# Two tiles for the image of the first pass, other homes for the second pass's first buffers

## The chip, the cores and the metric

The kernel runs on one core of a Trainium2 chip. The metric is device time in microseconds (us), the median of three runs. The engines named below are PE (TensorE, matrix products), DVE (VectorE), ACT (ScalarE), POOL (GpSimd) and SP (SyncE, which here only issues DMAs). "PEld" in the profile is the load of a matmul's stationary operand.

## What is computed

Two layers over `x` of shape (8, 256, 64, 64) in float32, eight images of 256 channels and 4096 pixels:

```python
# layer 0: attention of all pixels to 256 reduced positions
xr = conv(x, w_sr, stride 4x4)            # 16x16 positions
xr = layer_norm(xr)
q = w_q @ x;  k, v = split(w_kv @ xr)     # 8 heads of 32
out = softmax(q k^T / sqrt(32)) v
x = x + gamma * (w_out @ out)

# layer 1: linear attention on qkv and on a convolved copy
qkv = w_qkv @ x                           # 768 channels
agg = grouped_1x1(depthwise_5x5(qkv))     # 96 groups of 8
for each head of 8 channels in (qkv, agg):
    q, k = relu(q), relu(k);  kv = sum over pixels of k (v, 1)
    att = (q kv) / (q sum(k) + 1e-15)
p = batch_norm(w_proj @ att)              # 512 -> 256
return x + p
```

## The kernel before

There are three passes. Each writes to scratch memory in DRAM what the next one reads.

**The first pass** does layer 0 and the `qkv` product of layer 1. It goes over the eight images b, each in 8 strips of 512 pixels. An image's `x` is one tile `x_b` of 128 partitions x 2 x 4096 numbers, 32 KB in each partition; there are two such homes, used in turn (`xpools`, L583), so `x_{b+2}` lies where `x_b` lay. `load_x` (L600) queues eight loads, one for each strip (`load_strip`, L605). `keys_values` (L675) reduces the image by 1024 matmuls of `sr` over all pixels (L687), a line in the profile. `queries` (L759) and `added` (L842) work on a strip: `added` writes layer 0's result over `x_b` and stores it to `x2` in DRAM (L850, two stores for each strip). After two strips, a group, `differences` (L856) and the products of `qkv` (L891) make the `qkv` of the group; its parts go out by way of `stage` tiles to `planes` (L924), and by way of `turned` tiles to `k` (L934) and `v` (L939). An image has four groups, so the last group's stores come after strip 7's `x2` stores.

**The second pass** does the depthwise convolution and the sums over pixels, in 64 units; unit u stands for a half t, a quarter k of the half and an image b, with b running fastest. Unit u needs the tiles

- `d1_u` and `d0_u`, 578 KB each, from `planes` (`load_cells`, L1126);
- `kq_u`, 512 KB, from `k`, and `vq_u`, in four loads of 384 KB, from `v` (`load_tokens`, L1133 and L1143);
- `w1` and `w0`, the convolution's weights, four loads of 384 KB each for eight units (`load_weights`, L1120).

`paired` makes `c1_u` from `d1_u` by two subtractions on DVE (L1153, L1154) and a copy on POOL (L1157); `positive` (L1196) takes the relu of `kq_u` on ACT and reduces it on POOL (`red_raw`). `convolve(u, 1, i)` makes three banks `cv1_u_2`, `cv1_u_0`, `cv1_u_1` with 8 matmuls each (L1213), which become `r1_u` by `both` (L1220, ACT), `s` (L1228, DVE) and a relu (L1229, ACT). `summed_raw` (`raw_u`, L1238) multiplies `kq_u` and `vq_u`, `summed` (`sums_u`, L1255) `r1_u` and `vq_u`; `ended` (`few_u`, L1298) and `ended_raw` (L1285) finish them with the reduced tiles `red_agg_u` and `red_raw_u`. `convolve(u, 0, i)` (with L1217) does the same for the queries and `applied` (`ng_u`, L1329) multiplies them by the sums; `stored` (L1349) writes the result `att_u`. Work on a unit reaches over four turns of the main loop (L1353): `cv1_u` in its own, `sums` one later, `cv0` two later, `ng` three later.

Before its loop the pass queues `w1` of the first eight units, `d1_0`, `kq_0`, `vq_0`, then `w0`, then the constants `taps` (1152 KB), `mix`, `msk`, `rep_w` and `pix` (L1169) with `d1_1` between them, then `d0_0`. `kq_1` and `vq_1` are queued in the loop's first turn.

**The third pass** does the normalisation of layer 1 on the first half of its heads (`n`, L1526), transposes both halves (`at`, L1544) and projects (`p`, L1562), in 64 steps. It begins with a mask, `vec` and `wproj` (the projection's weights), the sums `kvp` of the first images (L1436), and `raw` (L1458) and `xs` (L1467) for each step; the first `n`, `at` and `p` mix with the second pass's last units.

**What sets the order.** Nothing writes the order of instructions out by hand: a scheduler places them on the engines by priorities that follow the program, and an instruction can only be placed when the memory of the tile that it writes has been released. All loads and stores stand in one queue that SP works off in order: an issue that waits holds back everything behind it. A DMA also waits for the one eight places before it to land. Tiles of the second pass lie on memory that the first pass has used: a pool of the second pass takes addresses in the order in which the pools are opened (L1097 and after), so a tile's home decides which tile of the first pass must be through before its load can stand in the queue, and the load's place in the queue follows from that. Two small tiles at the end of the first pass, `both` and `fits` (L1073 to L1081), test the range of some numbers for a slower path that these inputs do not take.

Of the kernel before, what the change touches and what calls it, by code (L numbers as in the profile page):

```python
# [574 lines left out]
def first_pass(ctx: ExitStack, tc: tile.TileContext, a, fine, planes, x2d, kd, vd, wtd):  # L575
# [2 lines left out]

    const = ctx.enter_context(tc.tile_pool(name="const", bufs=1))
    nilpool = ctx.enter_context(tc.tile_pool(name="nilpool", bufs=1))  # L580
    xpools = [ctx.enter_context(tc.tile_pool(name=f"xpool{i}", bufs=1)) for i in range(2)]
    keys = ctx.enter_context(tc.tile_pool(name="keys", bufs=1))
    two = ctx.enter_context(tc.tile_pool(name="two", bufs=2))  # L583
    made = ctx.enter_context(tc.tile_pool(name="made", bufs=1))
    rest = ctx.enter_context(tc.tile_pool(name="rest", bufs=2))
    halves = ctx.enter_context(tc.tile_pool(name="halves", bufs=1))

# [4 lines left out]
        return psum.tile([P, 512], F32, tag="mm", name=name, bufs=5)  # L592

    def load(src, name):
        consts[name] = const.tile(list(src.shape), F32, tag=name, name=name)
        nc.sync.dma_start(consts[name], src)

    consts, x_tiles = {}, {}

    def load_x(b):  # L600
        x_tiles[b] = xpools[b % 2].tile([P, 2, HW], F32, tag="x", name=f"x_{b}")
        for s in range(NG):
            load_strip(b, s)

    def load_strip(b, s):  # L605
        src = a.xp[b].rearrange("(c p) n -> p c n", p=P)
        cols = slice(s * QB, (s + 1) * QB)
        nc.sync.dma_start(x_tiles[b][:, :, cols], src[:, :, cols])

    def load_consts():  # L610
        for n, src in (
# [61 lines left out]
    kks, vvs = {}, {}  # L673

    def keys_values(b):  # L675
        xt = x_tiles[b]
        ln = lambda name: keys.tile([P, 2, NK], F32, tag="ln", name=f"{name}_{b}", bufs=3)
        xr = ln("xr")

# [2 lines left out]
        for f, tap in taps:  # L682
            w = keys.tile([P, 2, C], F32, tag="wsr", name=f"wsr_{b}_{f}", bufs=4)
            nc.sync.dma_start(w, a.w_sr[:, :, tap])
            for ci in range(2):
                for oc in range(2):
                    nc.tensor.matmul(  # L687
                        ps[:, oc],
                        w[:, ci, oc * P : (oc + 1) * P],
                        xt[:, ci, f * NK : (f + 1) * NK],  # L690
                        start=(f == ci == oc == 0),
                        stop=(f == R * R - 1 and ci == 1),
                        skip_group_check=True,
                    )
            yield
# [60 lines left out]
    def queries(b, s, c):  # L756
        ps = bank(f"q_{b}_{s}_{c}")
        for ci in range(2):
            nc.tensor.matmul(  # L759
                ps,  # L760
                consts["wq"][:, ci, c * P : (c + 1) * P],
                x_tiles[b][:, ci, s * QB : (s + 1) * QB],
                start=(ci == 0),
                stop=(ci == 1),
            )
        qs = two.tile([P, QB], F32, tag="q", name=f"q_{b}_{s}_{c}")
        nc.scalar.copy(qs, ps)
        return qs
# [71 lines left out]
        late.append(noted)  # L840

    def added(b, s, att, oc):  # L842
        xt, cols = x_tiles[b], slice(s * QB, (s + 1) * QB)
# [3 lines left out]
        nc.vector.scalar_tensor_tensor(  # L847
            xt[:, oc, cols], ps, consts["gam"][:, 0:1], xt[:, oc, cols], ALU.mult, ALU.add
        )
        nc.sync.dma_start(x2d[b][oc * P : (oc + 1) * P, cols], xt[:, oc, cols])  # L850

    quarters = {}

    def differences(b, g):  # L856
        xt = x_tiles[b]
        x = xt[:, :, 2 * g * QB : 2 * (g + 1) * QB].rearrange("p c (h n) -> p c h n", h=2)
# [123 lines left out]


    weights = conv_weights()
    x_tiles[0] = xpools[0].tile([P, 2, HW], F32, tag="x", name="x_0")
    ahead = keys_values(0)
    for s in range(NG):
        load_strip(0, s)
# [81 lines left out]
        pass  # L1070


    both = const.tile([P, 2], F32, tag="both", name="both")  # L1073
    nc.vector.tensor_reduce(both, seen.rearrange("p (n k) -> p k n", k=2), AX.X, ALU.add)
    total = bank("total")[:, :2]
    nc.tensor.matmul(total, mean_w, both, start=True, stop=True)
    fits = const.tile([P, 4], F32, tag="fits", name="fits")
# [11 lines left out]
def second_pass(ctx: ExitStack, tc: tile.TileContext, a, planes, kd, vd, wtd, kvd, attd):  # L1089
    nc = tc.nc  # L1090
    B = a.x.shape[0]
    def pool(name, bufs=1):
        return ctx.enter_context(tc.tile_pool(name=name, bufs=bufs))

    const, late, mid = pool("const2"), pool("late2", 2), pool("mid2")  # L1097
    first, second, small, w_taps, pairs, sides, between, third, w_q, two = (
        pool("first2"), pool("second2"), pool("small2", 2), pool("taps2"), pool("pairs2", 2),
        pool("sides2", 2), pool("between2", 2), pool("third2"), pool("wq2"), pool("two2", 2),  # L1100
    )
    psums = {
        tag: ctx.enter_context(tc.tile_pool(name=f"psum_{tag}", bufs=1, space=bass.MemoryType.PSUM))
# [11 lines left out]
    def load_weights(u, what, g):  # L1115
        t, k, b = units[u]
        if g == 0:
            home = (third if k % 2 else first) if what else (third if k % 2 else w_q)
            wt[t, k, what] = home.tile([P, 4, 6 * P], F32, tag=f"w{what}_{k % 2}", name=f"w{what}_{t}_{k}")
        nc.sync.dma_start(wt[t, k, what][:, g], wtd[2 * what + t][:, 4 * k + g])  # L1120

    def load_cells(u, what):
        t, k, b = units[u]
        home = (second if u % 2 else first) if what else third
        d = home.tile([P, 4, (NB + 1) ** 2], F32, tag=f"d{what}_{u % 2}", name=f"d{what}_{u}")
        nc.sync.dma_start(d, planes[b, 2 * what + t][4 * k : 4 * k + 4].rearrange("g p e -> p g e"))  # L1126
        grids[u, what] = d.rearrange("p g (y x) -> p g y x", x=NB + 1)


    def load_tokens(u):  # L1130
        t, k, b = units[u]
        kq = (second if u % 2 else first).tile([P, 2, 4, P], F32, tag=f"kq_{u % 2}", name=f"kq_{u}")
        nc.sync.dma_start(  # L1133
            kq.rearrange("p a c e -> p a (c e)"),
            kd[b][4 * t + k].rearrange("a y (m i) b e -> (y m) a (i b e)", i=2),
        )
        kqs[u] = kq
        vq = (second if u % 3 else first).tile([P, 4, 6 * P], F32, tag=f"vq_{u % 3}", name=f"vq_{u}")
        v = vd[b][4 * t + k]
        row = (NB2 + 2) * P  # L1140
        for r in range(4):
            src = [[2 * row, NB], [4 * P, NB // 2], [1, 6 * P]]
            nc.sync.dma_start(vq[:, r], bass.AP(tensor=v.tensor, offset=v.offset + r * row, ap=src))  # L1143
        vqs[u] = vq.rearrange("p r (c f h e) -> p r c f h e", c=6, f=4, h=4)
# [16 lines left out]
        load_weights(0, 1, g)  # L1161
    load_cells(0, 1)
    load_tokens(0)
    for g in range(4):
        load_weights(0, 0, g)

    def load(home, src, name):
        t = home.tile(list(src.shape), F32, tag=name, name=name)
        nc.sync.dma_start(t, src)  # L1169
        return t  # L1170

    taps = load(w_taps, a.w_taps, "taps")
    load_cells(1, 1)
    mix = load(const, a.w_mix, "mix")
    msk = load(const, a.mask_h, "msk")
    rep_w = load(const, a.replicate, "rep_w")
# [24 lines left out]
    def convolve(u, what, i):  # L1201
# [14 lines left out]
                        out = out.rearrange("p (y x) -> p y x", y=NB)  # L1216
                    nc.tensor.matmul(out, m, x, start=(da == 0), stop=(da == 1))  # L1217
        if i == 2:
            both = between.tile([P, QB], F32, tag="both", name=f"both{what}_{u}")
            nc.scalar.copy(both, ps)  # L1220

            r = (sides if what else two).tile([P, 2, 4, P], F32, tag=f"r{what}", name=f"r{what}_{u}")
            state[u, what] = (r, both)
            (kts if what else qs)[u] = r
        else:
            r, both = state[u, what]
            s = sides.tile([P, QB], F32, tag="s", name=f"s{what}_{u}_{i}")
            nc.vector.tensor_add(s, ps, both)  # L1228
            nc.scalar.activation(r[:, i].rearrange("p h n -> p (h n)"), s, AF.Relu)  # L1229
# [18 lines left out]
    def summed(u):  # L1248
# [508 lines left out]
```

## Time and profile before

| | us |
|---|---|
| median of three runs | 3973.13 (3971.51 to 3975.15) |
| the profiled execution | 3977.62 |
| its span | 3975.8 |
| first pass, up to its last matmul | 2066 |
| second pass, its first `c1` to its last `ng` | 2042 to 3318 |
| third pass, to the end | 3291 to 3976 |

The mean granted clock of TensorE is 0.989 of full speed over the span. The passes overlap at their joints, as their instructions mix there.

The profile is of one execution. Its page gives busy time by engine, then the span in 40 slices, the DMA queues, the chain that ended last, the costliest groups of instructions and the DMA issues. In a timeline a line is a run of like instructions: start, length, engine, line of the code, operation, tiles, and in brackets the idle time before it and what ended it. In the list of waits a line is an engine and line, what it waited for, the total in us, how many times, and the longest. Loads of constants are counted by size:

```
vq<-v SPq DMA_DIRECT2D x256, 384.0 KB
d<-planes SPq DMA_DIRECT2D x128, 578.0 KB
x<-in_xp_dram SPq DMA_DIRECT2D x64, 512.0 KB
kq<-k SPq DMA_DIRECT2D x64, 512.0 KB
taps<-in_w_taps_dram SPq DMA_DIRECT2D x1, 1152.0 KB
mix<-in_w_mix_dram SPq DMA_DIRECT2D x1, 256.0 KB
```

### The profile page before, as it was taken

The numbers are of one execution on the slowest core, as the hardware profiler recorded it, in microseconds if no ns is written. First come the engines' busy times: TensorE is split into PE (matmuls) and PEld (weight loads), VectorE is DVE, ScalarE is ACT, GpSimd is POOL, SyncE is SP. The second block draws the span as 40 slices with busy tenths as digits, with TensorE's granted clock in tenths as the row PEclk, the third lists the DMA queues.
The fourth block names the chain that finished last, engine by engine and source line by source line (L and its number), as shares of the span: only waits on it lengthen the run. The fifth ranks groups of instructions, "written<-read, shape, count | busy, mean of one in ns | idle before, by whom it ended". The sixth has DMA issues, their size and how long they took to land. (4 is left out here: it accounts for less than half of the span.)

```text
span 3975.8 us, 70172 instructions
## 1 busy us (share of the span) xinstructions
PE 3884.2 (98%) x27074; PEld 2279.0 (57%) x27074; DVE 2267.2 (57%) x3752; ACT 1516.5 (38%) x3473; POOL 1291.5 (32%) x1394
## 2 busy tenths in 40 slices
PE   8999999999999999999988999999999998999998
PEld 4443434434344343443337888888888886555555
DVE  2567465564655646556664566666666664444444
ACT  2334344443444434444422222222222223555554
POOL 2344243342433424334433444444444430000000
PEclk9999999999999999999998999999999999999999
DMA  7655445344453444534549878878777657767674
GB/s 241 188 167 157 143 112 151 102 111 142 112 152 101 112 140 112 151 102 113 135 121 272 240 224 228 229 215 231 230 216 231 204 151 188 232 202 230 203 227 140
DMA packets 569897, 691.37 MB, mean 174 GB/s; under 512 B 60112, under 2 KB 429264, under 8 KB 565328
## 3 DMA queue, kind: packets, MB, share of 16 engines
q1 hardware_dynamic: 569552, 686.78, 60.9%
q8 instruction: 215, 3.52, 0.4%
q14 instruction: 130, 1.06, 0.1%
HBM read 412.54 MB, written 274.10 MB: 173 GB/s over the span
## 5 line engine op out<-in xcount | busy, mean ns | idle before, releaser
L809 POOL TENSOR_TENSOR e<-e,e 128x512 f32<-128x512 f32 x512 | 679.3, 1357 | 941.9 <-PE av L798 879.1
L780 ACT ACTIVATE e<-sc 128x512 f32<-128x512 f32 x1024 | 531.2, 603 | 803.1 <-PE sc L774 798.9
L1213 PE MATMUL cv<-w,c 128*128 128x128 f32 x3072 | 386.8, 280 | 11.4 <-POOL c L1157 11.0
L1213 PEld LDWEIGHTS cv<-w,c 128*128 128x128 f32 x3072 | 360.9, 193 | 42.3 <-issue 28.9
L1580 DVE TENSOR_TENSOR y<-z,xs 128x256 f32<-128x256 f32 x256 | 144.2, 652 | 312.8 <-ACT z L1571 300.1
L774 PE MATMUL sc<-q,kk 32*128 32x512 f32 x2048 | 320.1, 640 | 2.0 <-DVE part L960 1.0
L1255 PE MATMUL sums<-vq,r 128*32 128x288 f32 x4096 | 308.0, 414 | 0.0
L891 PE MATMUL qkv<-differences,combined 128*128 128x512 f32 x576 | 306.8, 624 | 0.9 <-ACT e L780 0.7
L907 DVE TENSOR_TENSOR whole<-part,qkv 128x512 f32<-128x512 f32 x256 | 175.5, 687 | 193.1 <-PE qkv L891 181.9
L798 PE MATMUL av<-e,vv 128*32 128x512 f32 x2048 | 273.1, 605 | 1.9 <-ACT att L818 1.9
L1229 ACT ACTIVATE r<-s 128x512 f32<-128x512 f32 x256 | 160.5, 627 | 299.9 <-DVE s L1228 299.7
L1571 ACT ACTIVATE z<-p,bn 128x256 f32<-128x256 f32 x256 | 133.7, 578 | 314.6 <-PE p L1562 240.4
L1217 PE MATMUL cv<-c,w 128*128 128x128 f32 x2048 | 253.4, 277 | 0.0
L1562 PE MATMUL p<-att,wproj 128*128 128x512 f32 x512 | 249.4, 609 | 1.9 <-ACT att L1545 1.9
L846 PE MATMUL o<-att,wout 128*128 128x512 f32 x512 | 234.4, 600 | 11.9 <-DVE att L831 11.9
L1220 ACT COPY both<-cv 128x512 f32<-128x512 f32 x128 | 74.9, 585 | 446.4 <-PE cv L1213 389.0
L759 PE MATMUL q<-x,wq 128*128 128x512 f32 x512 | 244.8, 600 | 0.0
L687 PE MATMUL sr<-x,wsr 128*128 128x256 f32 x1024 | 233.3, 382 | 9.3 <-DMA wsr<-in_w_sr_dram 9.3
L1562 PE MATMUL p<-agg,wproj 128*128 128x512 f32 x512 | 242.3, 596 | 0.0
L1217 PEld LDWEIGHTS cv<-c,w 128*128 128x128 f32 x2048 | 239.7, 192 | 0.0
L687 PEld LDWEIGHTS sr<-x,wsr 128*128 128x128 f32 x1024 | 195.5, 191 | 62.2 <-issue 33.6
L1228 DVE TENSOR_TENSOR s<-cv,both 128x512 f32<-128x512 f32 x256 | 171.9, 672 | 82.3 <-PE cv L1217 43.2
(143 smaller groups left out, 6030.8 us busy)
## 6 DMA issues: line engine op xcount, KB each, us to landing
vq<-v SPq DMA_DIRECT2D x256, 384.0 KB
planes<-stage SPq DMA_DIRECT2D x128, 578.0 KB
d<-planes SPq DMA_DIRECT2D x128, 578.0 KB
raw<-planes SPq DMA_DIRECT2D x128, 272.0 KB
x<-in_xp_dram SPq DMA_DIRECT2D x64, 512.0 KB
wsr<-in_w_sr_dram SPq DMA_DIRECT2D x128, 256.0 KB
x<-x SPq DMA_DIRECT2D x128, 256.0 KB
k<-turned SPq DMA_DIRECT2D x256, 128.0 KB
```

The source lines that it names most:

```text
L687: nc.tensor.matmul(ps[:, oc], w[:, ci, oc * P : (oc + 1) * P], xt[:, ci, f * NK : (f + 1) * NK], start=(f == ci == oc == 0), stop=(f == R ...
L759: nc.tensor.matmul(ps, consts["wq"][:, ci, c * P : (c + 1) * P], x_tiles[b][:, ci, s * QB : (s + 1) * QB], start=(ci == 0), stop=(ci == 1),)
L774: nc.tensor.matmul(scs[h], kks[b][rows, c, kc * P : (kc + 1) * P], qs[rows], start=True, stop=True)
L780: nc.scalar.activation(e, scs[h], AF.Exp, scale=D0**-0.5)
L798: nc.tensor.matmul(sums["av"][cols], vvs[b][:, kc, c * P + h * D0 : c * P + (h + 1) * D0], es[h], start=(kc == 0), stop=(kc == 1),)
L809: nc.gpsimd.tensor_tensor(es1[h], es0[h], es1[h], ALU.add)
L846: nc.tensor.matmul(ps, consts["wout"][:, c, oc * P : (oc + 1) * P], att[c], start=(c == 0), stop=(c == 1))
L891: nc.tensor.matmul(ps, w, x, start=True, stop=True)
L1213: nc.tensor.matmul(out, x, m, start=(da == 0), stop=(da == 1))
L1217: nc.tensor.matmul(out, m, x, start=(da == 0), stop=(da == 1))
L1255: nc.tensor.matmul(ps[h * D0 : (h + 1) * D0, : 36 * D1].rearrange("p (r n e) -> p r n e", r=3, e=D1), kt[:, par, h, 2 * r + c], vq[:, r : ...
L1562: nc.tensor.matmul(ps.rearrange("p (f q n) -> p f q n", f=4, q=4), wproj[:, j, oc * P : (oc + 1) * P], src, start=(j == 0), stop=(j == 3),)
```

## The change

`x` of an image becomes two tiles, one for strips 0 to 5 and one for strips 6 and 7, with two homes each; `strips(b, s, n)` gives the part for a strip. Code that used `xt[:, :, cols]` uses it, and computes the same. In the second pass `load_cells(1, 1)` and `load_tokens(1)` are called before `w0`'s loads and no longer after `taps` and in the loop; `taps` becomes two tiles, one for each half t. The pools are opened in another order, and several tiles get other homes: `d1`, `kq` and one of three `vq` of odd units lie in a pool of their own, `odd`; odd `d0` and the second half of `taps` in `more`; odd `w1` and `r1` in `second`; odd `w0` in `third_w`. `r1` has its two homes in two pools in place of a pool with two. In the first pass `made` is opened before `two`, and `wsmall`, `both` and `fits` move to other pools.

```diff
-    xpools = [ctx.enter_context(tc.tile_pool(name=f"xpool{i}", bufs=1)) for i in range(2)]
+    xpools = [[ctx.enter_context(tc.tile_pool(name=f"xpool{i}{j}", bufs=1)) for j in range(2)] for i in range(2)]
     keys = ctx.enter_context(tc.tile_pool(name="keys", bufs=1))
+    made = ctx.enter_context(tc.tile_pool(name="made", bufs=1))
     two = ctx.enter_context(tc.tile_pool(name="two", bufs=2))
-    made = ctx.enter_context(tc.tile_pool(name="made", bufs=1))
...
-        consts[name] = const.tile(list(src.shape), F32, tag=name, name=name)
+        consts[name] = (nilpool if name == "wsmall" else const).tile(list(src.shape), F32, tag=name, name=name)
...
+    def new_x(b):
+        x_tiles[b] = [
+            pool.tile([P, 2, n * QB], F32, tag="x", name=f"x{i}_{b}")
+            for i, (pool, n) in enumerate(zip(xpools[b % 2], (6, 2)))
+        ]
+
+    def strips(b, s, n=1):
+        t, at = (x_tiles[b][0], s) if s < 6 else (x_tiles[b][1], s - 6)
+        return t[:, :, at * QB : (at + n) * QB]
...
     def load_x(b):
-        x_tiles[b] = xpools[b % 2].tile([P, 2, HW], F32, tag="x", name=f"x_{b}")
+        new_x(b)
         for s in range(NG):
             load_strip(b, s)
...
-        nc.sync.dma_start(x_tiles[b][:, :, cols], src[:, :, cols])
+        nc.sync.dma_start(strips(b, s), src[:, :, cols])
...
-                        xt[:, ci, f * NK : (f + 1) * NK],
+                        strips(b, f // 2)[:, ci, f % 2 * NK : (f % 2 + 1) * NK],
...
-    both = const.tile([P, 2], F32, tag="both", name="both")
+    both = halves.tile([P, 2], F32, tag="both", name="both")
...
-    const, late, mid = pool("const2"), pool("late2", 2), pool("mid2")
-    first, second, small, w_taps, pairs, sides, between, third, w_q, two = (
-        pool("first2"), pool("second2"), pool("small2", 2), pool("taps2"), pool("pairs2", 2),
-        pool("sides2", 2), pool("between2", 2), pool("third2"), pool("wq2"), pool("two2", 2),
+    late, const = pool("late2", 2), pool("const2")
+    first, second, small, mid, odd, w_taps, pairs, sides, between, third, third_w, w_q, two, more = (
+        pool("first2"), pool("second2"), pool("small2", 2), pool("mid2"), pool("odd2"), pool("taps2"),
+        pool("pairs2", 2), pool("sides2", 2), pool("between2", 2), pool("third2"), pool("third_w2"), pool("wq2"),
+        pool("two2", 2), pool("more2"),
     )
...
-            home = (third if k % 2 else first) if what else (third if k % 2 else w_q)
+            home = (second if k % 2 else first) if what else (third_w if k % 2 else w_q)
...
-        home = (second if u % 2 else first) if what else third
+        home = (odd if u % 2 else first) if what else (more if u % 2 else third)
...
-        kq = (second if u % 2 else first).tile([P, 2, 4, P], F32, tag=f"kq_{u % 2}", name=f"kq_{u}")
+        kq = (odd if u % 2 else first).tile([P, 2, 4, P], F32, tag=f"kq_{u % 2}", name=f"kq_{u}")
...
-        vq = (second if u % 3 else first).tile([P, 4, 6 * P], F32, tag=f"vq_{u % 3}", name=f"vq_{u}")
+        vq = (first, odd, second)[u % 3].tile([P, 4, 6 * P], F32, tag=f"vq_{u % 3}", name=f"vq_{u}")
...
     load_cells(0, 1)
     load_tokens(0)
+    load_cells(1, 1)
+    load_tokens(1)
     for g in range(4):
         load_weights(0, 0, g)
...
-    taps = load(w_taps, a.w_taps, "taps")
-    load_cells(1, 1)
+    taps = []
+    for t in range(2):
+        taps.append((more if t else w_taps).tile([P, 4, 36, D1], F32, tag="taps", name=f"taps_{t}"))
+        nc.sync.dma_start(taps[t], a.w_taps[:, 4 * t : 4 * t + 4])
...
-            both = between.tile([P, QB], F32, tag="both", name=f"both{what}_{u}")
+            both = (between if what else late).tile([P, QB], F32, tag="both", name=f"both{what}_{u}")
...
-            r = (sides if what else two).tile([P, 2, 4, P], F32, tag=f"r{what}", name=f"r{what}_{u}")
+            home = (second if u % 2 else sides) if what else two
+            r = home.tile([P, 2, 4, P], F32, tag=f"r{what}", name=f"r{what}_{u}", bufs=2 - what)
...
-        nc.vector.tensor_mul(p, ps[:, : 36 * D1].rearrange("p (n e) -> p n e", e=D1), taps[:, 4 * t + k])
+        nc.vector.tensor_mul(p, ps[:, : 36 * D1].rearrange("p (n e) -> p n e", e=D1), taps[t][:, k])
...
-        if u + 1 < n_all:
+        if 0 < u < n_all - 1:
             load_tokens(u + 1)
```

What the scheduler makes of it: every engine has the same instructions as before, but for one DMA more (`taps` in two). `x` loads of strips 0 to 5 of images 2 to 7 stand right behind the `x2` stores of strip 7 of the image two before; those of strips 6 and 7 stay where all eight stood. `d1_1`, `kq_1` and `vq_1` stand where `taps` stood, ahead of all of image 7's stores; `taps_0`, `mix`, `msk`, `rep_w` and `pix` among the stores of images 0 and 1; `taps_1` where `d1_1` stood. On PE `cv1_1` stands directly behind `cv1_0`, ahead of `raw_0`. On DVE the subtractions of `c1_1` and the sums `s1_1` come before the first pass's last additions to `stage`. At the third pass's beginning `vec` and `wproj` are queued behind the store of `att_63_0`, and `kvp_1`'s first addition stands behind `tok_3_1` on DVE, where `tok_3_1` stood behind it.

More of the change, by code (lines that the diff above doesn't have):

```diff
@@ L675, in keys_values @@
     def keys_values(b):
-        xt = x_tiles[b]
         ln = lambda name: keys.tile([P, 2, NK], F32, tag="ln", name=f"{name}_{b}", bufs=3)
@@ L761, in queries @@
                 consts["wq"][:, ci, c * P : (c + 1) * P],
-                x_tiles[b][:, ci, s * QB : (s + 1) * QB],
+                strips(b, s)[:, ci],
                 start=(ci == 0),
@@ L842, in added @@
     def added(b, s, att, oc):
-        xt, cols = x_tiles[b], slice(s * QB, (s + 1) * QB)
+        xt, cols = strips(b, s), slice(s * QB, (s + 1) * QB)
         ps = bank(f"o_{b}_{s}_{oc}")
@@ L847, in added @@
         nc.vector.scalar_tensor_tensor(
-            xt[:, oc, cols], ps, consts["gam"][:, 0:1], xt[:, oc, cols], ALU.mult, ALU.add
+            xt[:, oc], ps, consts["gam"][:, 0:1], xt[:, oc], ALU.mult, ALU.add
         )
-        nc.sync.dma_start(x2d[b][oc * P : (oc + 1) * P, cols], xt[:, oc, cols])
+        nc.sync.dma_start(x2d[b][oc * P : (oc + 1) * P, cols], xt[:, oc])
     quarters = {}
     def differences(b, g):
-        xt = x_tiles[b]
-        x = xt[:, :, 2 * g * QB : 2 * (g + 1) * QB].rearrange("p c (h n) -> p c h n", h=2)
+        x = strips(b, 2 * g, 2).rearrange("p c (h n) -> p c h n", h=2)
         b11, b12, b21, b22 = (x[:, c, h] for c in range(2) for h in range(2))
@@ L984, in first_pass @@
     weights = conv_weights()
-    x_tiles[0] = xpools[0].tile([P, 2, HW], F32, tag="x", name="x_0")
+    new_x(0)
     ahead = keys_values(0)
@@ L1076, in first_pass @@
     nc.tensor.matmul(total, mean_w, both, start=True, stop=True)
-    fits = const.tile([P, 4], F32, tag="fits", name="fits")
+    fits = halves.tile([P, 4], F32, tag="fits", name="fits")
     nc.vector.tensor_scalar(fits[:, 0:1], total[:, 0:1], SUM_MAX / D0 / C, None, ALU.is_le)
```

## The prediction

> **What bounds the kernel now.** I read first the busy time of each engine, then the waits of PE, then the PE timeline where those waits stand, then SP's own issue times and busy time by window there.
>
> ```profile
> PE 3884.2 (98%) x27074; PEld 2279.0 (57%) x27074; DVE 2267.2 (57%) x3752; ACT 1516.5 (38%) x3473; POOL 1291.5 (32%) x1394
> ...
> PE cv L1213 <- POOL c L1157: 11.0, 2, 10.0
> ...
> PE raw L1238 <- issue: 6.9, 1, 6.9
> ...
> PE few L1298 <- POOL red_agg L1191: 5.4, 1, 5.4
> PE ng L1329 <- ACT r L1229: 5.0, 1, 5.0
> ```
>
> PE is busy 98% of the span. No PE instruction is added or dropped, so the time can fall only by PE's idle time and by matmuls that ran at half clock. The waits (total, times, longest) stand mostly at the joints between passes.
>
> ```profile
> 2066.57 1.14 PE L1213 MATMUL cv<-w,c 128*128 128x128 f32 x8
> 2074.65 1.08 PE L1238 MATMUL raw<-vq,kq 128*32 128x32 f32 x64 [6.94 <-issue]
> 2076.17 5.68 PE L1255 MATMUL sums<-vq,r 128*32 128x288 f32 x64
> ...
> 2092.13 7.70 PE L1213 MATMUL cv<-w,c 128*128 128x128 f32 x48 [9.97 <-POOL c L1157]
> 2105.34 0.59 PE L1298 MATMUL few<-ones,red_agg 128*128 128x1 f32 x2 [5.36 <-POOL red_agg L1191]
> ```
>
> These are unit 0 and unit 1 of the second pass: PE idles 6.94 us before `raw_0`, 9.97 us before `cv1_1`, 5.36 us before `few_1`; with 0.97 us behind that, 23.24 us in 40. A further 4.94 us stands at 2171.40, before the `raw` of unit 6, which waits for its `kq`. Who is late:
>
> ```profile
> 2081.80 1.17 SPq L924 DMA_DIRECT2D planes<-stage  x2
> 2083.07 1.71 SPq L1126 DMA_DIRECT2D d<-planes  x1
> 2088.43 1.77 SPq L1120 DMA_DIRECT2D w<-wt  x4
> 2090.24 0.55 SPq L1169 DMA_DIRECT2D mix<-in_w_mix_dram  x1
> ...
> 2093.70 0.38 SPq L1133 DMA_DIRECT2D kq<-k  x1
> 2095.02 2.83 SPq L1143 DMA_DIRECT2D vq<-v  x4
> 2097.90 0.59 SPq L1126 DMA_DIRECT2D d<-planes  x1
> ```
>
> SP's queue is in order. `d1_1` stands behind the last `planes` stores, and everything that units 1 and 2 need stands behind it.
>
> ```profile
> 2088.40:2108.60 20.20, 10.14 (x122) 9.86 (x126) 6.86 (x12) 3.09 (x5) 8.23 (x9) 0.67 1.00 302
> 2108.60:2170.00 61.40, 57.86 (x730) 48.35 (x726) 34.13 (x65) 14.83 (x27) 25.35 (x29) 0.96 1.03 274
> 2180.00:2320.00 140.00, 139.24 (x1782) 122.29 (x1782) 82.20 (x164) 39.36 (x74) 55.20 (x65) 1.00 0.86 237
> ```
>
> In each line (window, length, busy time of PE, PEld, DVE, ACT, POOL, granted clock, DMA share, GB/s) the DMA share is the second number from the end. It is full until 2170 us and PE follows the transfers; past 2180 PE is full again.
>
> **Unit 1's loads and the constants.** `d1_1`, `kq_1` and four `vq_1` (578+512+1536 KB) go to where `taps` stood, at 1779.6 us, ahead of image 7's stores. `taps_0`, `mix`, `msk` go behind image 1's first `x2` stores, which SP issued at 368.57 before a pause until 375.65; 834 KB at the rate below are 3.3 us, so the pause covers them (without it, 3.3 us of SP once). `rep_w` and `pix` (72 KB) follow at some 402, ahead of 408.95's next issue. `taps_1` (576 KB) takes `d1_1`'s place. So 330+512+1536 = 2378 KB, 2.435 MB, are gone between the last store and `d1_2`. What such bytes cost I take from the same stretch: from `w0`'s issue at 2088.43 to POOL's copy of `c1_2` at 2108.68, 1536+330+578+512+1536+578 = 5070 KB, 5.19 MB, went in 20.2 us, 257 GB/s. 2.435 MB at that rate are 9.5 us; at the best rate in the trace that I found (eight `x` loads of 512 KB landing 1.35 us apart at 1643 to 1652.6, 388 GB/s) 6.3. From 2088.43, `w0`, `d0_0` and `d1_2` are 2.76 MB, 10.7 us: `d1_2` lands at about 2099.
>
> PE in the new order: `cv1_1`, 24 matmuls at full clock some 2x1.95+2.03 = 5.9 us (48 records took 7.70 at half clock), stands right behind `cv1_0`, in the old gap of 6.94. `raw_0` still waits for a PSUM bank that DVE's last `stage` adds free (2074.43), which now stand behind `s1_1`; about 2 us of gap stay. Then `sums_0`, `raw_1`, `few_0`, `sums_1`, `few_1` follow, and PE arrives at `cv1_2` between 2091 and 2095, to wait for `d1_2`, its copy and POOL's clock: it starts at about 2100, where it started at 2114.96. That alone would be 15 us. But units 2 to 6 stand in the same full queue, whose bytes are only 9.5 us earlier, and the 4.94 us at `raw_6` show that it still sets the pace at 2170. So 15 is the bound and **-9.5** the term; the rest reappears as waits between 2105 and 2170. The lower bound is the 6.3.
>
> A rule to set beside this: the Trainium skill, "DMA: Bandwidth & Descriptors", section Specifications, gives about 358 GB/s as what one core gets from HBM; by it alone the bytes would be worth 6.8 us, an estimate. The `x` loads' 388 GB/s go past that figure, so the measured rates stand. The second, "TensorE: Matmul & The Clock Gate", Part 1, says that about 3.4 us of idleness halve the clock, which speaks against a full gain while one gap stays ahead of `cv1_2`. The trace agrees that clock falls with idleness: 0.67 mean in the 20 us around the two gaps, 1.00 from 2180; by the rule the sum would be -10 in place of -12, as the 7.70 us against 5.9 return; by the row, one gap in place of three leaves less at half clock than before, and I add nothing.
>
> **The first pass.** `x` of an image is two tiles (strips 0 to 5, strips 6 and 7). The six loads of the first are queued right behind the `x2` stores of strip 7, so ahead of the last group's `planes`, `k` and `v` stores; before, all eight stood behind these. For images 0 to 5 SP so issues 6x512 KB earlier, each about 0.6 us of its own time (8 took 4.82) and 1.35 us landing (eight landed 1643.2 to 1652.6). The stores behind them come due next:
>
> ```profile
> 1830.61 2.49 SPq L850 DMA_DIRECT2D x<-x  x2
> 1848.22 0.52 SPq L924 DMA_DIRECT2D planes<-stage  x1
> ```
>
> SP has 15.5 us between the end of one and the start of the other (image 6, with no loads there); six loads need 4.8 us to the first landing and 5x1.35 more, 11.6. The cover holds: **0**; each microsecond beyond 15.5 would come six times. At the front of image 7, unit 1's six issues have 1779.98 to 1794.65; 2.69 MB at 257 GB/s are 10.5 us: covered too.
>
> DVE gets `c1_1`'s two subtractions (L1153, 0.72 us each) in the last `qkv` work, where it is 14.23 us busy of 16 (2050 to 2066); on its heels come the last stores. Price between 0 and 1.4 us, I take **+0.5**, as 11% of that stretch is free and PE there is bound by itself (16.00 of 16).
>
> **The third pass.** The joint at 3290 to 3370 us is reordered by the same homes. `kvp_1`'s add moves behind `tok_3_1`; before, `tok` stood behind it on DVE while it waited for its DMA:
>
> ```profile
> 3363.39 0.30 DVE L1436 TENSOR_TENSOR kvp<-kvp 128x132 f32<-128x132 f32 x1 [4.71 <-DMA kvp<-kv]
> 3364.34 0.66 PE L1544 MATMUL at<-ident,tok 128*128 128x128 f32 x4 [3.19 <-DVE tok L1531]
> ```
>
> That is 3.19 us of PE, and the next user of `kvp_1` is an image later: -3.2 (0 to -3.2). `att_61_1`'s store goes ahead of the mask loads and `kvp_0`'s add ahead of the transposition that feeds it, so the 5.02 us before `ng` (3311.86) may shorten: -1.5, between 0 and -5. `vec` and `wproj` move from 3292 behind the store of `att_63_0` (3317.22) and ahead of `raw_1`. `p` starts at 3322.96. `wproj` (512 KB) would be issued near 3318.4; at the 4.82 us of the first `x` load it lands in time, at the 7.8 that `raw_1` took from 3317.80 it is 3.2 late: 0 to +4 with the issue times' looseness, I take +1.8. Net **-3**, between -8 and +4.
>
> **Sum.** -9.5 + 0 + 0.5 - 3 = -12, against 3977.62 us of the profiled execution (span 3975.8 and 1.8 around it): 3965.6. The median of three runs is 3973.13, 4.5 below the profiled one; from there **3961 us**. A measurement of this kernel tells some 0.2%, 8 us, from no change; -12 is faster.
>
> **The rivals.**
>
> *PE keeps its early start.* If the transfers after `d1_2` are not what paces units 2 to 6 (share 1.03 falls to 0.86 when work and loads are steady), the 15 us stay: -15 + 0.5 - 3 to -8 = -17 to -23, 3950 to 3956. Against it: the wait for `kq_6`. Chance 0.2.
>
> *The backlog hides it.* The full queue gives back only the 6.3 us of the best rate, and the third pass pays for `wproj` without the gains: -6.3 + 0.5 + 1.8 = -4 at one end, -6.3 + 1.4 + 4 = -1 at the other, 3969 to 3972. For it: DMA is past its share of 1.0 until 2170. Chance 0.16.
>
> *Slower: loads ahead of stores.* The six `x` loads stand at the head of the queue in front of the last group's stores, and ACT, DVE and PE refill the stage buffers those stores empty. From the point where the loads take longer than 15.5 us, that is below 3.15 MB / 15.5 = 203 GB/s, PE waits once per image. At 151 GB/s, a whole slice's mean in the page's row of the first pass, they take 20.9 us: 6x(20.9-15.5) = 32, less 12: 3993. Against it: that slice's DMA share is 0.5, and the eight loads at 1643 ran at 388 GB/s. Chance 0.06.
>
> *The change does not do it.* `w0` waits at 2088.43 for the last `planes` store to land, and with unit 1 in place early the gap before `cv1_2` could stay as long. But 2.4 MB behind that point are gone whatever happens, so this ends in the second rival.
>
> **Chances.** Forecast 0.58 (3957 to 3966), early start 0.2, backlog 0.16, slower 0.06. Faster by over 0.2% (below 3965.2): 0.2 and nearly all of the forecast, 0.77; within: 0.17; slower: 0.06. Range 3951 to 3969: it leaves out the far end of each rival.
>
> **What would show it.** A gap of about 2 us before `raw_0` with `cv1_1` ahead of it; one wait of `cv` on `c`, 5 to 9 us, at about 2100, in place of 9.97 and 5.36; small waits for `kq` before 2170; the gap of 3.19 us at 3364 gone; `ng`'s 5.02 shorter; `x` loads right behind strip 7's stores, with PE without gaps in the first pass. I am wrong if PE shows waits of over 2 us in each image, if `cv1_2` starts after 2105, or if units 3 to 6 show no waits (then the early start is kept).

## The result, and the profile after

Over 22 runs each the changed kernel takes 3963.98 us (3959.67 to 3968.55) and the kernel before 3971.72 us (3965.51 to 3977.88). The ratio is 0.998, with a 95% interval of 0.9974 to 0.9987: 5.2 to 10.3 us faster. The forecast was 12 us, 3961; range and sign hold, the size is two thirds of it.

The two profiled executions differ by more, 17 us (span 3975.8 and 3958.8), and the first thing to learn is why they may not simply be subtracted. Four points of PE's timeline in both, in us from the start of the span:

| | before | after | difference |
|---|---|---|---|
| first `q` of image 1, strip 2 | 363.14 | 355.46 | -7.7 |
| last `qkv` product of the first pass | 2065.33 | 2057.55 | -7.8 |
| first `sums` of unit 7 | 2228.55 | 2213.52 | -15.0 |
| first `p` of step 60 | 3930.60 | 3913.08 | -17.5 |

Between the first two rows nothing changes at all, in 1700 us. The 7.7 us arise in the first 360. Of these, 6.4 are there already at the first `q` of image 1, strip 0 (303.6 and 297.2 us), and up to it every engine and the queue do the same in the same order: only the homes of tiles differ. The experiments show below that this start wanders from execution to execution, and that it goes with TensorE's granted clock. What the change does is in the rest: 7.3 us at the joint of passes one and two, 2.5 behind it, 9.7 in these two profiles.

PE's waits after the change (what it waited for, total us, times, longest; line numbers in a view are those of that run's own kernel):

```profile
PE cv L1227 <- POOL c L1167: 10.5, 2, 9.5
...
PE raw L1253 <- ACT kq L1210: 5.7, 1, 5.7
PE p L1577 <- DMA wproj<-in_w_proj_dram: 5.6, 1, 5.6
...
PE ng L1344 <- ACT r L1244: 3.4, 1, 3.4
```

The entry of 6.9 us for `raw` and that of 5.4 for `few` are gone. One wait of `cv` for `c` remains, `ng`'s 5.0 is 3.4, and a wait for `wproj` is new. PE's timeline (start, length, idle time before):

```profile
2067.31 0.75 PE L1253 MATMUL raw<-vq,kq 128*32 128x32 f32 x64 [2.02 <-ACT r L1244]
...
2083.95 0.41 PE L1320 MATMUL few<-m,rep_w 128*128 128x36 f32 x2 [1.92 <-DVE m L1288]
2093.82 5.64 PE L1227 MATMUL cv<-w,c 128*128 128x128 f32 x26 [9.46 <-POOL c L1167]
...
2155.84 1.08 PE L1253 MATMUL raw<-vq,kq 128*32 128x32 f32 x64 [5.71 <-ACT kq L1210]
```

`raw_0` has 2.02 us of gap in place of 6.94, as `cv1_1` now runs ahead of it. `cv1_2` starts 36.3 us behind the last `qkv` where it started at 49.6 (2114.96 less 2065.33). But 62 us later stands the old wait before a `raw`, 5.71 us long where it was 4.94. Busy time by window (PE, PEld, DVE, ACT, POOL, clock, DMA share, GB/s) says why:

```profile
2081.40:2101.60 20.20, 8.59 (x109) 7.75 (x103) 5.93 (x11) 1.82 (x3) 6.35 (x8) 0.66 0.99 291
2101.60:2155.00 53.40, 46.88 (x567) 40.74 (x567) 29.01 (x55) 13.26 (x25) 19.89 (x22) 0.99 1.03 274
2170.00:2310.00 140.00, 140.00 (x1858) 122.13 (x1860) 86.98 (x163) 40.98 (x77) 60.13 (x69) 1.00 0.85 237
```

DMA is as full up to the last wait as it was before the change, and PE is full without a gap behind it. So the end of that wait is where the joint ends.

**Which load it is.** The wait's name, `kq`, misleads, and it misled the prediction too. The `raw` in question is that of unit 5, and `kq_5` had landed at 2135.4. The relu of `kq_5` on ACT (2154.75) stands behind a relu of `r0`, which waits for `s0` on DVE, which stands behind this:

```profile
2149.74 0.72 DVE L1163 TENSOR_TENSOR c<-d 128x544 f32<-128x544 f32 x1 [3.28 <-DMA d<-planes]
2150.39 1.22 DVE L1164 TENSOR_TENSOR c<-d 128x544 f32<-128x544 f32 x1
...
2153.53 1.25 DVE L1243 TENSOR_TENSOR s<-cv,both 128x512 f32<-128x512 f32 x2
```

`c1_6` waits for `d1_6`, a tile of the next unit, and three engines wait in line behind it. In the kernel before it is the same tile, 15.5 us later:

```profile
2165.28 0.73 DVE L1153 TENSOR_TENSOR c<-d 128x544 f32<-128x544 f32 x1 [5.33 <-DMA d<-planes]
...
2169.08 1.25 DVE L1228 TENSOR_TENSOR s<-cv,both 128x512 f32<-128x512 f32 x2
```

Taken from the last `qkv` of each, `d1_6` lands at 99.9 us before and at 92.1 after. That is the quantity which the experiments follow.

### The profile page after: what moved, and what is told of

It reads as the page before. It is cut to its first block, busy times and chain, and to the rows that moved or that the text cites. A ratio compares the mean times of both kernels' runs of the same rounds, so it can differ in the third digit from the quotient of the medians.

```text
span 3958.8 us, 70047 instructions
## 1 busy us (share of the span) xinstructions
PE 3876.3 (98%) x27074; PEld 2277.0 (58%) x27074; DVE 2271.4 (57%) x3752; ACT 1517.6 (38%) x3473; POOL 1296.6 (33%) x1394
## 5 line engine op out<-in xcount | busy, mean ns | idle before, releaser
L1234 ACT COPY both<-cv 128x512 f32<-128x512 f32 x128 | 75.0, 586 | 409.0 <-PE cv L1227 355.5
```

## The experiments

The expectations call the `q` of image 1, strip 2, the sixth queries, counted in pairs of strips. For each kernel the table gives two distances from the last `qkv` product of the first pass, which leave the wandering start out: to the first `sums` of unit 7 and to the first `p` of step 60. `d1_6` is its landing on the same scale, and GB/s the bytes of all loads and stores queued between the last `planes` store and `d1_6`, over the time from the one's landing to the other's. Times are medians; ratios are to the kernel before, timed in turn with it.

| kernel | `sums_7` | step 60 | `d1_6` | GB/s | time, us (runs) | ratio, 95% interval |
|---|---|---|---|---|---|---|
| before | 163.2 | 1865.3 | 99.9 | 266 | 3971.7 (22) | |
| before, again (e8) | 161.0 | 1860.3 | 97.5 | 276 | 3973.0 (1) | |
| changed | 156.0 | 1855.5 | 92.1 | 264 | 3964.0 (22) | 0.998, 0.9974 to 0.9987 |
| changed, again (e11) | 155.4 | 1854.0 | 92.2 | 265 | 3960.3 (1) | |
| e1 unit 1 late | 162.8 | 1863.0 | 99.0 | 275 | 3972.3 (11) | 1.0004, 0.9995 to 1.0013 |
| e2 `x` behind | 155.5 | 1856.3 | 91.4 | 267 | 3964.8 (11) | 0.9982, 0.9972 to 0.9991 |
| e3 `taps_1` late | 151.9 | 1852.1 | 87.6 | 273 | 3965.5 (9) | 0.9978, 0.9968 to 0.9987 |
| e4 `d1_2` first | 154.0 | 1855.5 | 93.9 | 258 | 3963.8 (11) | 0.9978, 0.9969 to 0.9987 |
| e5 `wproj` early | 156.3 | 1857.2 | 93.3 | 258 | 3966.6 (12) | 0.9979, 0.997 to 0.9988 |
| e6 e3 and e5 | 154.6 | 1853.6 | 90.7 | 258 | 3963.5 (10) | 0.9973, 0.9963 to 0.9983 |
| e7 `d1_1` late | 155.1 | 1856.1 | 93.3 | 272 | 3963.9 (9) | 0.9979, 0.9967 to 0.999 |
| e7 again (e12) | 159.6 | 1859.6 | 96.1 | 261 | 3972.1 (1) | |
| e9 `w1` later | 156.0 | 1856.0 | 85.8 | 268 | 3963.3 (8) | 0.9975, 0.9964 to 0.9985 |
| e10 e9 and e3 | 149.6 | 1852.0 | 82.9 | 269 | 3959.4 (8) | 0.9972, 0.9962 to 0.9983 |

Two profiles of one program differ at `sums_7` by 0.6 (changed), 2.2 (before) and 4.5 us (e7); the intervals of the timings are 5 to 9 us wide.

### e1: unit 1's loads back behind the last stores

```diff
+    def behind(u, dma):
+        return tc.keep_in_program_order(dma) if u == 1 else dma
...
-        nc.sync.dma_start(d, planes[b, 2 * what + t][4 * k : 4 * k + 4].rearrange("g p e -> p g e"))
+        behind(u, nc.sync.dma_start(d, planes[b, 2 * what + t][4 * k : 4 * k + 4].rearrange("g p e -> p g e")))
...
     load_tokens(0)
+    taps = []
...
     load_cells(1, 1)
-    load_tokens(1)
...
-        if 0 < u < n_all - 1:
+        if u < n_all - 1:
             load_tokens(u + 1)
```

`load_tokens` has the same `behind`; `taps` is loaded ahead of `d1_1`, and `load_tokens(1)` is called in the loop as it was.

> Changed kernel, with unit 1's d1_1, kq_1 and vq_1 held in SP's queue behind taps_1, where they stood before; homes, split x and constants as changed. Theory 1 (the gain is the 2.1 MB that unit 1's loads take out of the queue behind the last stores): the joint of passes one and two loses most of its gain; the sums of unit 12 come about 8.3 us (2.1 MB at 257 GB/s) later against the last qkv work than in the changed kernel, and the time is about 3971, no different from before by 2 us. Theory 2 (the gain stands in the first pass, where the changed profile was 7.7 us ahead by 363 us): the time stays near 3964 to 3966 and the first 363 us are as in the changed profile.

Measured: 3972.29 us, a ratio of 1.0004. All of the gain is gone, though homes, split `x` and early constants are there; `sums` of unit 12 come 6.8 us later than in the changed kernel (8.3 were expected). The gaps are back where they were:

```profile
2070.75 1.08 PE L1255 MATMUL raw<-vq,kq 128*32 128x32 f32 x64 [7.14 <-issue]
...
2089.76 8.17 PE L1229 MATMUL cv<-w,c 128*128 128x128 f32 x48 [9.80 <-POOL c L1170]
```

The start of this kernel is queued as in the changed one. Its interval against the kernel before runs from 2 us faster to 5 us slower, so what else the change does in the first pass brings at most 2 of the 7.7 us, on average.

### e2: the `x` loads back behind the last group's stores

```diff
-        nc.sync.dma_start(strips(b, s), src[:, :, cols])
+        dma = nc.sync.dma_start(strips(b, s), src[:, :, cols])
+        if b > 1:
+            tc.keep_in_program_order(dma)
```

> Changed kernel, with the six x loads of strips 0 to 5 held behind the last group's stores as before; order on PE, DVE, ACT and POOL is unchanged. Theory 1: their place costs and brings nothing, time 3964 within 2 us, the q matmuls of images 2 to 7 keep a constant distance to those of the changed profile. Theory 2 (early x loads or what else differs in the first pass brings the 7.7 us): 3970 or more, and the loss shows between 150 and 363 us or once in each image.

Measured: 3964.78. From the sixth queries to the last `qkv` the two profiles agree to 0.1 us. The early `x` loads neither cost nor bring anything: theory 1.

### e3: less in the queue

```diff
-    for t in range(2):
+
+    def load_taps(t):
         taps.append(...)
...
+    load_taps(0)
...
+        if u == 12:
+            tc.keep_in_program_order(load_taps(1))
```

> Changed kernel, with the second half of taps (576 KB, 0.59 MB) loaded in the turn of unit 12 and no longer right behind the last stores; order on the other engines unchanged. Theory 1 (bytes in that queue set the pace up to unit 6): d1_2 lands 2.3 us earlier (0.59 MB at 257 GB/s), the gap of 9.46 us before cv1_2 falls to about 7.2, and units 6 and later come some 2 us earlier: time 3962. Rival (what paces there is not bytes but when the last planes store has landed, for which w0 waits): w0 and d1_2 are issued at the same time, gap and time unchanged, 3964.

Measured:

```profile
2099.87 4.94 PE L1230 MATMUL cv<-w,c 128*128 128x128 f32 x26 [7.35 <-POOL c L1167]
```

The gap before `cv1_2` is 7.35 us, as the bytes have it (7.2), while `w0`'s issue stands 6.1 us behind that of the last `planes` store as before. The rival falls. `sums_7` comes 4.1 us earlier, more than the 2.3 expected; in e6, with the same edit, it is 1.6 us earlier than in e5. So 0.59 MB brought between 1.6 and 4.1 us in single profiles. The timing, 3965.5 where 3962 was expected, does not resolve it.

### e4: the same bytes in another order

```diff
-    for g in range(4):
-        load_weights(0, 0, g)
...
+    load_cells(2, 1)
+    for g in range(4):
+        load_weights(0, 0, g)
```

The second block stands behind `paired(0, 1)`, ahead of `taps` and `d0_0`, and the loop's `load_cells(2, 1)` goes.

> Changed kernel, with d1_2 queued ahead of w0 and taps_1, so the same bytes in another order. Theory 1 (the queue sets the pace up to unit 6): the gap of 9.46 us before cv1_2 falls to 3 to 5, but kq_2, vq_2 and w0 are as late as before, other gaps grow by as much, and the sums of unit 7 come within 1.5 us of the changed kernel's: 3963 to 3964. Rival (PE keeps an early start): 5 us or more are kept at unit 7, 3959.

PE's timeline:

```profile
2095.25 5.06 PE L1220 MATMUL cv<-w,c 128*128 128x128 f32 x22 [2.78 <-POOL c L1167]
...
2181.32 1.08 PE L1246 MATMUL raw<-vq,kq 128*32 128x32 f32 x64 [7.41 <-ACT kq L1203]
```

The gap before `cv1_2` falls from 9.46 to 2.78, and `sums_5` comes 12.1 us earlier. At the next unit's `raw` 7.41 us are waited. Against the two profiles of the changed kernel `sums_7` is ahead by 2.0 and 1.4 (up to 1.5 was expected), `sums_12` by 0.05 and behind by 0.5. An earlier start of PE was worth nothing here, with the queue behind it as long. This is the clearest of the runs.

It speaks against another rival as well, TensorE's clock. Over the 120 us behind the last `qkv` the mean granted clock is 0.87 in both profiles before and in e1, and 0.90 and 0.91 in the two of the changed kernel, so the gain could have been one of the clock. In e4 it is 0.93, and `sums_12` comes no earlier.

### e5 and e6: `wproj` early

```diff
-    data, flattened, results = (
-        ctx.enter_context(tc.tile_pool(name=name, bufs=2)) for name in ("data3", "flattened3", "results3")
+    data, flattened, wide, results = (
+        ctx.enter_context(tc.tile_pool(name=name, bufs=1 if name == "wide3" else 2))
+        for name in ("data3", "flattened3", "wide3", "results3")
...
-    wproj = const.tile([P, 4, C], F32, tag="wproj", name="wproj")
+    wproj = wide.tile([P, 4, C], F32, tag="wproj", name="wproj")
```

`vec` goes with `wproj`; e6 adds e3's edit.

> Changed kernel, with vec and wproj of the third pass in a pool of their own behind flattened3, so that their loads are queued 20 places earlier, ahead of the loads for unit 63's d0. Theory 1 (the late wproj takes back most of what the reordered joint of passes two and three brings): the wait of 5.56 us before the first p goes, and the first 'at' of step 16 or later comes 3 to 5 us earlier against sums of unit 63; time 3960. But kvp_1's addition stands ahead of tok_3_1 again here, so up to 3.2 us may come back there. Rival (the first p has to wait for att and q anyway, as in the kernel before): other waits take its place, less than 1.5 us gained.

> Changed kernel with two of the earlier edits at once: the second half of taps loaded in unit 12's turn, and vec and wproj early. If both act at their own joint, the stretch from the last qkv to the last p is shorter than in the changed kernel by 3.5 (as the run with taps alone showed) plus what the run with wproj alone shows; 3957 at 3 to 4 for the second. Rival: the joint of passes two and three starts with other loads in flight and the parts do not add.

Measured in e5, first on PE and then on ACT:

```profile
3311.75 1.32 PE L1542 MATMUL n<-kvm,q 128*128 128x144 f32 x4 [6.60 <-ACT q L1507]
```

```profile
3310.91 0.78 ACT L1507 ACTIVATE q<-raw 128x256 f32<-128x256 f32 x2 [5.63 <-DMA raw<-planes]
```

The wait for `wproj` is gone, and one of 6.60 us for `q`, so for a load of `raw`, stands in its place. From `sums_63` to step 60 it takes 644.0 us, and 641.9 in e6, which has a wait of 5.70 us for `q` there. The ten profiles with the changed third pass, whose `wproj` is late, take 642.1 to 644.3. So the rival holds within this scatter of some 2 us: another load of the same queue is late in place of `wproj`, and nothing is gained that the profiles can tell.

At step 60 e6 is 3.5 us ahead of e5, as e3 is 3.4 ahead of the changed kernel, so the two edits seem to add. But up to `sums_63`, where only the edit on `taps` can act, the lead is 1.5 in one case and 4.1 in the other; the rest of the 3.5 is the scatter at the last joint. That the ends agree is luck.

### e7 and e12: `d1_1` alone late

```diff
     load_tokens(0)
+    load_tokens(1)
+    taps = []
...
     load_cells(1, 1)
-    load_tokens(1)
```

Here only `load_cells` has the `behind` of e1.

> Changed kernel, with d1_1 alone (578 KB) held behind taps_1 and the last stores; kq_1 and vq_1 stay early. cv1_1 can then not fill the gap before raw_0. Theory 1 (bytes in the queue pay): the gap of 7 us before raw_0 is back, yet at the sums of unit 7 only the 0.59 MB are missing, 2.3 to 4.1 us later than in the changed kernel (the run without taps_1 showed 4.1 for 0.59 MB); time 3967. Rival (what pays is that cv1_1 runs in PE's idle time): 6 to 7 us later at unit 7, as when all of unit 1 came late; time 3971.

> The kernel with d1_1 alone late once more. If the first profile's lack of a loss (sums of unit 7 at 155.1 us, 0.9 before the changed kernel's) was a lucky transfer rate (272 GB/s against 258 to 267), this one stands at 157 to 159; if d1_1 costs nothing there, at 155 to 156 again.

PE in e7 has its gap before `raw_0` again, and one before `cv1_1`:

```profile
2068.15 1.08 PE L1256 MATMUL raw<-vq,kq 128*32 128x32 f32 x64 [7.24 <-issue]
...
2087.96 7.46 PE L1230 MATMUL cv<-w,c 128*128 128x128 f32 x48 [9.99 <-POOL c L1170]
```

Still `sums_7` comes at 155.1, as in the changed kernel, and the time is 3963.9, where theory 1 had 3967 and the rival 3971. The second profile gives 159.6. Their mean, 157.3, is 1.6 us behind the changed kernel's 155.7; 0.59 MB at 264 GB/s are 2.2. So the mean is near what the bytes say and far from the 6 to 7 of the rival: that `cv1_1` fills PE's gap seems to be worth little by itself. The first profile's lack of a loss goes with a rate of 272 GB/s, the second's loss with 261. With two profiles 4.5 us apart the exact price of `d1_1` stays open.

### e9 and e10: weights later

```diff
-            load_weights(u + B - b, 1 if b < 4 else 0, b % 4)
+            if u >= B:
+                load_weights(u + B - b, 1 if b < 4 else 0, b % 4)
+            elif u >= 4:
+                for g in {4: (0, 1), 5: (2,), 6: (3,), 7: ()}[u]:
+                    load_weights(B, 1, g)
+                load_weights(B, 0, u - 4)
```

e10 adds e3's edit.

> Changed kernel, with the four loads of w1 for units 8 to 15 (384 KB each) moved from the turns of units 0 to 3 to those of units 4 to 6, behind the load of d1_6. Theory 1, as the eight profiles so far have it: the joint ends when d1_6 lands, and that follows the bytes queued between the last planes store and it, at 258 to 276 GB/s; 1.57 MB less are 5.7 to 6.1 us. So d1_6 lands about 86 us behind the last qkv (changed kernel: 91.4 to 93.3), the wait of raw_5 falls from 5.7 to under 1, sums of unit 7 come 4 to 6 us earlier; time 3959. Rival (the bytes are a bystander and PE follows another chain): less than 2 us at unit 7.

> The same with the second half of taps loaded in unit 12's turn as well: 2.15 MB less ahead of d1_6. Theory 1: d1_6 lands 8 us earlier than in the changed kernel, but PE's waits up to unit 6 hold only some 19 us, of which the first 2 to 4 are no loads', so 6 to 8 us earlier at unit 7; time 3957. Rival: as above.

In e9 `d1_6` lands at 85.8, as expected, and `sums_7` does not come earlier at all. The wait has moved to unit 4. PE and DVE there:

```profile
2138.68 1.08 PE L1253 MATMUL raw<-vq,kq 128*32 128x32 f32 x64 [5.87 <-ACT kq L1210]
```

```profile
2131.80 0.73 DVE L1163 TENSOR_TENSOR c<-d 128x544 f32<-128x544 f32 x1 [6.01 <-DMA d<-planes]
...
2136.34 0.68 DVE L1243 TENSOR_TENSOR s<-cv,both 128x512 f32<-128x512 f32 x1
```

The scheduler's order on DVE is another one in this kernel: the subtraction of `c0_2` stands ahead of the first `s0_1`, so DVE waits for `d0_2`, and then 1.47 us for `d1_5`, with work for ACT and PE behind it. In the changed kernel that `s0_1` was done when DVE came to `c0_2`, and the wait for `d0_2` was short:

```profile
2129.25 0.73 DVE L1163 TENSOR_TENSOR c<-d 128x544 f32<-128x544 f32 x1 [0.99 <-DMA d<-planes]
```

But `d0_2` is late by itself too. With 1.18 MB less queued ahead of it, 4.4 us at 268 GB/s, it lands 72.0 us behind the last `qkv`; the two profiles of the changed kernel have it at 71.7 and 74.1. The stretch up to it ran at 252 GB/s in e9, against 276 and 265. So the bytes gave the landing of `d1_6` and not that of a load before it, and theory 1 was wrong on the time. How much of the loss is DVE's order and how much the lower rate, one profile can't say. It does show that another order moves the wait to another load.

In e10, with 0.59 MB less again, `d1_6` lands 9.2 us earlier than in the changed kernel (8 were expected), `sums_7` comes 6.4 us earlier, 4.7 are left at unit 8 and 3.5 at step 60. Its median, 3959.4, is the lowest of all; its interval overlaps the changed kernel's, so that it is faster than that one is likely and not shown by the timings.

### e8 and e11: the same kernels once more

> The kernel before once more, for a second profile. If the 7.7 us by which the changed profile was ahead at 363 us were an effect of the change, this profile has its sixth queries at 363 us, as the first one had, within 1 us; if the start of the run wanders from execution to execution, as the profiles of the changed kernel's variants suggest (355.5 to 364.1), it can stand anywhere there. From the sixth queries to the end it takes the same time as in the first profile, within 1 us.

> The changed kernel once more, for the scatter of a profile. Sums of unit 7 at 155.5 to 156.3 us behind the last qkv, as in the three profiles with its order there; sixth queries anywhere between 355 and 364 us.

The kernel before has its sixth queries at 363.14 us again. This alone would speak for an effect of the change; but e7 and e12 are one program and have it at 356.4 and 363.1. Of the 12 profiles with the changed kernel's first pass or nearly so, eight lie between 355.5 and 359.1 and four at 363.1 to 364.1. In e1, which starts as the changed kernel does and has the joint of the kernel before, the time is that of the kernel before to within 0.13%. So the start brings little or nothing on average; whether the kernel before ever has the early one, two profiles can't say.

The start goes with the granted clock. Its mean over the first 355 us is 0.962 to 0.976 in the eight early profiles, and 0.938 to 0.957 in the six late ones, the two of the kernel before among them at 0.957; from 360 us to the last `qkv` it is 1.000 in all. Whether the lower clock makes the late start, or PE's waits there make both, this does not tell.

Nor did the expected 1 us hold from there to the end: the second profile of the kernel before took 4.7 us less. Up to the last `qkv` the two agree to 0.1 us, 2.2 are gained up to unit 7, 1.1 more up to unit 12, and the rest behind `sums_63`. e11 has its `sums_7` at 155.4, where it was expected.

## Why the prediction was right, and where it was off

*What bounds the kernel.* Right in substance: PE outside the joints, the DMA queue at the joint until the last wait. The reading of that wait was wrong in its tile. It was put down to `raw` of unit 6 and its `kq`; it is unit 5's, and the late load is `d1_6`, two engines away.

*Unit 1's loads and the constants*, -9.5. The sequence came as told: 2.02 us before `raw_0` (about 2 forecast), `cv1_2` waiting for `d1_2`, an early start of 13.4 us of which the queue takes back half (15, of which 9.5 were to stay). Its wait is 9.46 us where 5 to 9 were forecast, and the small waits for `kq` are one of 5.71. The kept part is the term that was mis-sized. `sums_7` comes at 162.1 in the mean of the two profiles before and at 155.7 in the two after: -6.4, and at `sums_63` it is -7.5. The bytes are right, 2.44 MB. At the 271 GB/s that the two profiles before show over the whole 75 us up to `d1_6` they are 9.0 us, but the stretch left behind ran at 264 to 265, which gives back 1.7 in 68, and the last `planes` store landed 0.8 us later. Why the rate is lower, and if it is so in general, stays open: single profiles of all kernels lie between 258 and 276. The clock, for which nothing was added, rose from 0.87 to 0.90 and 0.91 over this stretch; e4 shows no gain from that.

The rule of the Trainium skill that was set beside it, 358 GB/s ("DMA: Bandwidth & Descriptors", Specifications), would have had 6.8 us, an estimate. That is nearer to the measured term, but not for its reason: the queue moved 258 to 276 GB/s in every profile here.

*The first pass.* The `x` loads at 0: right (e2). `c1_1` on DVE at +0.5: the last `qkv` stands where it stood, to 0.01 us from image 7's queries on, and the last `planes` store is issued 17.7 and 18.0 us behind it where it was 17.1 and 17.4. So 0.6, all of it in the stores. That `c1_1` is the reason is not shown: in e7 and e12, where `c1_1` comes late, the store is issued 18.5 and 18.6 us behind.

*The third pass*, -3. Wrong: from `sums_63` to step 60 it takes 643.7 and 642.0 us before, 642.6 and 642.1 after, and up to 644.3 in the other profiles with this third pass. So no gain is shown. The gains that were counted came (3.19 us before `at` gone, `ng` 5.02 to 3.39), and `wproj`, priced at +1.8 in bounds of 0 to 4, cost 5.56:

```profile
3303.03 1.29 PE L1559 MATMUL at<-ident,tok 128*128 128x128 f32 x8 [3.41 <-DVE tok L1546]
3309.88 3.75 PE L1577 MATMUL p<-att,wproj 128*128 128x512 f32 x4 [5.56 <-DMA wproj<-in_w_proj_dram]
```

Two waits that were not counted changed as well. One of `n` in the profile before is gone after, and `p`'s wait for `att` is 4.1 us in place of 1.9:

```profile
PE n L1526 <- ACT q L1491: 2.5, 2, 1.4
```

```profile
PE p L1577 <- ACT att L1560: 4.1, 2, 2.9
```

All of `at`, `ng`, `n` and `p` together, PE waits 16.0 us before and 16.5 after. The step that failed is adding gains and losses of single waits: as one goes another grows. e5 took the 5.56 away and got nothing that can be told.

*The rivals.* "PE keeps its early start" is refuted by e4, and "slower: loads ahead of stores" by the changed kernel's profile, where PE has no gap over 0.25 us between 336 and 1989 us, and by e2. "The backlog hides it" (3969 to 3972) gave too little, though its mechanism is the one that cut the forecast.

*The sum.* Against the profiled execution it was -12. Two profiles of each give 1862.8 and 1854.8 us from the last `qkv` to step 60, -8.0, and the medians -7.7. The time itself, 3964 where 3961 was forecast, looks closer than that by luck: the forecast started from a median of three runs that lies 1.4 us above the one of 22.

## What to carry to other kernels

Where a full queue sets the pace, count the bytes up to the last load that holds an engine up, and divide by the rate of that whole stretch; filling a compute engine's gap, or changing the order of the same bytes, only moved the wait here. Take the result as good to a few us: it gave 9.0 for the 6.4 measured, and in e9 some 6 where nothing came at unit 7. Follow a named wait back through the in-order queues of two or three engines before you price it: the tile in its name may have landed 20 us ago. And before two profiles are subtracted, find a stretch that both have in common and take distances from there, or a start that wanders is credited to the change.

## What was not expected of the hardware

One program, two executions (e7 and e12), the same stretch of the first pass:

```profile
160.00:240.00 80.00, 77.84 (x313) 36.48 (x308) 49.95 (x64) 26.11 (x62) 25.53 (x21) 1.00 0.60 187
```

```profile
160.00:240.00 80.00, 77.51 (x294) 35.81 (x287) 43.96 (x57) 24.62 (x58) 19.58 (x20) 0.91 0.54 173
```

PE is as busy, but the granted clock is 1.00 in the first and 0.91 in the second, which has 19 matmul records less. Between the `q` of strip 4 and that of strip 6 of image 0 the second loses 5.6 of the 6.8 us that lie between them at the sixth queries, nearly as much as all that the change brings. 9% of 80 us at full clock are 7.2 us, so the clock is enough to account for it. What lowers the clock in one execution and not in the other, the runs do not show.
